# A conv-sequence block with two attentions: the order of the time-score products, and the shape of two band-score blocks

## The chip, the core and the metric

The kernel runs on one core of a Trainium2 chip. The metric is the device time of one execution in microseconds, the median of several runs. The core has a matrix engine (PE, with its weight loads shown as PEld), a vector engine (DVE), a scalar engine (ACT), GpSimd (POOL) and a queue that starts transfers (SP). PE works on 128x128 cells, and a product may use a part of them: a tile of rows*columns. "32*64" is a tile of 32 rows (the depth of the product) and 64 columns (the partitions of its output).

## The reference, cut to what matters

The input x has the shape (2, 256, 128, 128): batch, time, band, channel, in float32. Two attentions with 4 heads of depth 32 follow each other, the first over the 256 times with a causal mask, the second over the 128 bands with a mask that leaves |i - j| <= 16. A feed-forward block ends it.

```
xt = ln(x, ...).transpose(0, 2, 1, 3)
x = x + mha(xt, t_wi, ..., h=4, mask=causal(256)).transpose(0, 2, 1, 3)
xf = ln(x, ...)
x = x + mha(xf, f_wi, ..., h=4, mask=band(128, 16))
xn = ln(x, ...)
x = x + (gelu(xn @ w1.T + b1) @ w2.T + b2)

# inside mha
scores = einsum('...hqd,...hkd->...hqk', q, k) / sqrt(32) + mask
o = einsum('...hqk,...hkd->...hqd', softmax(scores), v)
```

## The kernel before, in words

The work is cut into groups of 512 rows, `NT = 4` blocks of 128. There are 128 groups of time attention (`OverTime`, two sequences of 256 times each), then 128 of band attention (`OverBands`, four sequences of 128 bands) and 128 of feed-forward, the last two in alternating runs of eight. `BoundedPath.run` (line 1058) is a hand-written software pipeline: one turn of its loop issues pieces of several groups, and every engine executes what it is given in this order (`InOrder` pins it).

A time step issues on PE: the scores (`time_scores`), the row sums and weighted values of an earlier group (`weigh`: `p,ones` and `p,v`), the output product of a still earlier one (`output`: `wn,oT`), the queries and keys (`xnT,wf`) and the values (`wf,xnT`) of a later one. A band step has the same parts with `pf` in place of `p`.

Scores are made transposed, keys on partitions and queries along the free dimension, one product per head and half block of 64 keys. The row group of PE is the head (its 32 rows), the column half is that of the output's partitions; so there are eight 32*64 tiles, and products on different tiles can run beside each other. `first_scores` (line 678) makes, for a new group, the scores of the first 128 keys of a sequence against all 256 queries from the key on: 256 queries for the first half of the keys, 192 for the second. `second_scores` (line 686) makes, for the group before it, the second 128 keys against the second 128 queries: 64 and 128 queries, with the halves exchanged, so that each tile gets 256 + 64 or 192 + 128 columns per head and sequence. `time_scores` (line 741) interleaves both by a written list of head, kind and sequence, with both halves of each entry one after the other; 32 products in all.

Each head's scores have a bank of their own in PSUM: `a0` to `a3` for the first scores, `b0` to `b3` for the second. In a step these banks come from other work. After the exchange at the end of the loop's body (lines 1164 to 1169), `b1` is the bank that held the weighted values `op` of the step before, which DVE reads last (`oT`), and `b2` is the one with the new values `vp`, which ACT copies to `v`. `rp`, the row sums, is written into `b0` after the scores, when ACT has read the second scores of head 0 from it. ACT takes the exponentials in the order: second scores of heads 0 and 3, first scores of head 1, second of 1 and 2, first of 2, and later first of 0 and 3.

`OverBands.scores` (line 764) goes over the four sequences `i` and two halves `e` of 64 keys, and over the heads innermost: 32 products of 64 keys by 80 queries (the half and the 16 bands beside it), each on a 32*64 tile. What lies outside of the band is masked after the exponential, or before it for one head.

PE takes each float32 product in two passes, so that every product leaves two loads and two matmuls in the profile, and the counts there are twice those of the code.

Of the kernel before, what the change touches and what calls it, by code (L numbers as in the profile page):

```python
# [19 lines left out]
P = 128  # L20
H = 4
D = 32
BAND = 16
EPS = 1e-5
NEG = -1e38
NT = 4
# [6 lines left out]
HALF = P // 2  # L33
# [613 lines left out]
def rows_of(h):  # L647
    return slice(h * D, (h + 1) * D)
# [9 lines left out]
class OverTime(Attention):  # L658
# [16 lines left out]
        self.p1 = path.work.tile([P, 2, H, 2, P], F32, name="p1", tag="h", bufs=2)  # L675
        self.s1 = {h: path.bank([P, 2, P], "sp", path.banks[f"b{h}"]) for h in range(H)}

    def first_scores(self, h, s):
        r, a = rows_of(h), 2 * s * P
        for e in range(0, P, HALF):  # L680
            self.path.tensor.matmul(
                self.s0[h][e : e + HALF, s, e:], self.kT[r, a + e : a + e + HALF], self.qT[r, a + e : a + 2 * P],
                start=True, stop=True,
            )

    def second_scores(self, h, s):
        r, a = rows_of(h), (2 * s + 1) * P
        for e in range(0, P, HALF):
            q = P - HALF - e
            self.path.tensor.matmul(  # L690
                self.s1[h][e : e + HALF, s, q:], self.kT[r, a + q : a + q + HALF], self.qT[r, a + q : a + P],
                start=True, stop=True,
            )

    def first_weights(self, heads):
        for h in heads:
# [41 lines left out]
        self.rp = rp.rearrange("p s n q -> p (s n q)")  # L738


def time_scores(old, new):


    if new is not None:
        new.first_tiles()
    if old is not None:
        old.second_tiles()
    for h, second, s in (
        (0, 1, 0), (1, 0, 0), (2, 0, 0), (3, 1, 0), (0, 1, 1), (3, 1, 1), (0, 0, 0), (3, 0, 0),
        (1, 0, 1), (2, 0, 1), (0, 0, 1), (3, 0, 1), (1, 1, 0), (2, 1, 0), (1, 1, 1), (2, 1, 1),  # L750
    ):
        if second and old is not None:
            old.second_scores(h, s)
        if not second and new is not None:
            new.first_scores(h, s)


class OverBands(Attention):
# [5 lines left out]
    def scores(self, heads):  # L764
        path = self.path
        self.sp = {h: path.bank([P, NT * P], "sp") for h in heads}
        for i in range(NT):
            for e in range(2):
                keys = slice(e * HALF, (e + 1) * HALF)
                a = i * P + e * (HALF - BAND)  # L770
                q = slice(a, a + HALF + BAND)
                for h in heads:
                    r = rows_of(h)
                    path.tensor.matmul(
                        self.sp[h][keys, q], self.kT[r, i * P + e * HALF : i * P + (e + 1) * HALF], self.qT[r, q],
                        start=True, stop=True,
                    )

    def first_function(self):
# [107 lines left out]
class BoundedPath:  # L887
# [170 lines left out]
    def run(self, x, out):  # L1058
# [21 lines left out]
        for n in range(-12, len(groups) + 2):  # L1080
# [10 lines left out]
            if old is not None or new is not None:  # L1091
                time_scores(old, new)
                b = self.banks
                Attention.place = dict(rp=b["b0"], op=b["b3"], yp=b["a1"], qp=b["a2"], kp=b["b1"], vp=b["b2"])
            else:
                Attention.place = {}
# [142 lines left out]
```

## Time and profile before

| | |
|---|---|
| median of 3 runs | 2707.29 us (2706.91 to 2709.16) |
| the profiled execution | 2709.79 us |
| its span, first to last instruction | 2708.0 us |
| time stage | up to about 980 us |
| band and feed-forward stage | from there to the end |
| `bank<-qT,kT`, all scores | 16384 matmul records, of them 8192 with 80 columns |
| mean of one record of 64, 80, 128, 192, 256 columns | 223, 244, 277, 331, 386 ns |

The page has the span, the busy time of each engine and its share, and the groups of instructions. "Busy" of PE counts the time in which at least one matmul is in flight, and a record runs from the start of a matmul to its end in the pipe; records of several tiles overlap. A timeline merges instructions that follow each other with the same operands: start, length, engine, line, operation, output and inputs, tile, shape, count, and in brackets the idle time before it and what ended it. Line 882 is the helper through which every pinned instruction goes, so groups are told apart by tile names.

### The profile page before, as it was taken

What the parts mean: (1) busy time and instruction counts of PE and PEld (TensorE: products, weight loads), DVE (VectorE), ACT (ScalarE), POOL (GpSimd) and SP (SyncE); (2) the same over time, 40 slices, a digit from 0 to 9 for tenths busy, and PEclk for the clock granted to TensorE, in tenths of its full rate; (3) what the DMA queues carried; (4) which work ended last, traced back from release to release, by engine and by line L of the source; (5) the groups of instructions that cost most, each with busy time, mean ns of one, the idle gap of its engine ahead of it and who ended that gap; (6) DMA issues with size and microseconds to landing.
All of it is one profiled execution on the core that took longest, in us unless ns stands there. A gap on an engine that the chain in (4) does not pass through costs nothing.

```text
span 2708.0 us, 156754 instructions
## 1 busy us (share of the span) xinstructions
PE 2670.3 (99%) x68662; PEld 1826.6 (67%) x68662; DVE 2176.8 (80%) x6708; ACT 1858.2 (69%) x3620; POOL 1952.8 (72%) x2297
## 2 busy tenths in 40 slices
PE   8999999999999999999999999999999999999998
PEld 5766666666766666666666666666666667666665
DVE  7888888888888898868779678687697796886974
ACT  6888888888888874755746647557456465575563
POOL 4888888888888887667657666676576666665762
PEclk9999999999999999999999999999999999999999
DMA  5555555555555535445454454454444444544533
GB/s 147 152 148 145 149 148 141 150 146 146 150 141 149 145 95 137 109 117 135 106 127 124 114 130 110 120 133 111 124 126 113 124 118 120 130 113 123 128 100 82
DMA packets 471513, 347.10 MB, mean 128 GB/s; under 512 B 43297, under 2 KB 405153, under 8 KB 470817
## 3 DMA queue, kind: packets, MB, share of 16 engines
q1 hardware_dynamic: 469568, 335.92, 48.2%
q8 instruction: 540, 8.85, 1.5%
q14 instruction: 157, 1.28, 0.2%
q10 hardware_dynamic: 1248, 1.05, 0.1%
HBM read 169.03 MB, written 167.77 MB: 124 GB/s over the span
## 4 chain that ended last, share of the span: by engine, by line
PE 81%; DVE 14%; DMA 2%; issue 1%; SPq 1%; ACT 0%; DVEq 0%; ACTq 0%
PE bank L882 81%; DVE xh L882 3%; DVE bank L882 3%; DVE z L882 2%; DVE stats L882 2%; DVE u L882 2%; DVE x L882 1%; DMA xnT<-turned 1%; DVE mv L882 1%; DMA turned<-z 1%; SPq L882 1%; DMA x<-in_x 0%; DVE oT L882 0%; DMA rows_sb<-in_rows 0%; ACT p L882 0%
## 5 line engine op out<-in xcount | busy, mean ns | idle before, releaser
L882 ACT ACTIVATE hT<-bank,b 128x512 f32<-128x512 f32 x512 | 347.0, 688 | 535.8 <-PE bank L882 517.7
L882 POOL TENSOR_SCALAR_AFFINE_SELECT pf<-pf 128x512 f32<-128x512 f32 x768 | 478.6, 637 | 248.1 <-ACT pf L882 221.7
L882 DVE TENSOR_SCALAR xh<-x,mv,rstd 128x160 f32<-128x160 f32 x1536 | 596.9, 431 | 14.3
L882 PEld LDWEIGHTS bank<-w2T_sb,hT 128*32 128x32 f32 x16384 | 459.7, 110 | 63.3 <-issue 39.7
L882 PE MATMUL bank<-xnT,wf 128*32 128x512 f32 x4096 | 489.1, 592 | 2.5 <-ACT p L882 2.5
L882 PE MATMUL bank<-w2T_sb,hT 128*32 128x128 f32 x16384 | 477.7, 273 | 1.1 <-issue 0.8
L882 PE MATMUL bank<-xnT,w1f 128*32 128x512 f32 x4096 | 474.8, 592 | 0.0
L882 DVE TENSOR_TENSOR res<-bank,res 128x512 f32<-128x512 f32 x256 | 175.9, 687 | 338.9 <-PE bank L882 337.7
L882 POOL TENSOR_SCALAR_AFFINE_SELECT p<-p 128x1024 f32<-128x1024 f32 (+2 forms) x384 | 364.8, 950 | 109.9 <-ACT p L882 101.4
L882 ACT ACTIVATE p<-bank 128x512 f32<-128x512 f32 (+1 forms) x1024 | 417.4, 499 | 21.7 <-PE bank L882 4.1
L882 PE MATMUL bank<-qT,kT 32*64 32x80 f32 (+4 forms) x16384 | 351.7, 274 | 3.7 <-DVE oT L882 2.4
L882 PEld LDWEIGHTS bank<-wf,xnT 128*32 128x32 f32 x8192 | 236.0, 110 | 153.9 <-issue 101.2
L882 PEld LDWEIGHTS bank<-qT,kT 32*64 32x64 f32 x16384 | 295.7, 130 | 58.9 <-ACT kT L882 48.0
L882 POOL TENSOR_TENSOR p<-p,p 128x512 f32<-128x512 f32 x256 | 324.1, 1287 | 10.7
L882 DVE BATCH_NORM_STATS2 stats<-x 128x6 f32<-128x128 f32 x1536 | 326.5, 275 | 0.6 <-DMA x<-in_x 0.6
L882 ACT ACTIVATE pf<-bank 128x512 f32<-128x512 f32 x512 | 267.0, 602 | 50.9 <-PE bank L882 48.9
L882 PEld LDWEIGHTS bank<-xnT,w1f 128*32 128x32 f32 x4096 | 156.4, 110 | 189.9 <-issue 160.3
L882 DVE STREAM_TRANSPOSE z<-xh 128x512 f32<-128x512 f32 x384 | 273.3, 712 | 13.5
L882 POOL TENSOR_SCALAR rstd<-mv 128x4 f32<-128x4 f32 x248 | 56.7, 229 | 311.7 <-DVE mv L882 310.3
L882 PE MATMUL bank<-wn,oT 128*32 128x128 f32 x8192 | 273.2, 273 | 0.0
L882 PE MATMUL bank<-wf,xnT 128*32 128x128 f32 x8192 | 273.0, 273 | 0.0
L882 POOL TENSOR_TENSOR rstd<-rstd,mhalf 128x4 f32<-128x4 f32 x248 | 257.0, 1036 | 20.7
(97 smaller groups left out, 3656.3 us busy)
## 6 DMA issues: line engine op xcount, KB each, us to landing
turned<-z SPq DMA_DIRECT2D x1536, 64.0 KB, 2.5
xnT<-turned SPq DMA_DIRECT2D x384, 256.0 KB, 3.2
x<-in_x SPq DMA_DIRECT2D x128, 256.0 KB, 4.4
x<-res SPq DMA_DIRECT2D x256, 128.0 KB, 2.4
x<-x SPq DMA_DIRECT2D x128, 256.0 KB, 4.3
out<-res SPq DMA_DIRECT2D x256, 128.0 KB, 2.5
w1T_sb<-in_w1T ACTq DMA_DIRECT2D x1, 256.0 KB, 6.6
w2T_sb<-in_w2T ACTq DMA_DIRECT2D x1, 256.0 KB, 8.0
```

Of the source, the lines that this page charges most:

```text
L882: return self.tc.keep_in_program_order(emit(*args, **kwargs))
```

## The change

Two things change. The time scores are issued one half at a time, by a list `TIME_ORDER` of 32 entries: the kind (`s` second, `f` first), the head, the sequence and the half. The products are the same as before, only their order differs: the two halves of a pair no longer stand side by side, and the kinds are mixed differently.

In the band scores, the first and last sequence keep their products of 64 keys by 80 queries. The second and third become one product per head of 128 keys by 128 queries each, over all 128 columns of PE (a 32*128 tile). So a group has 24 products in place of 32: 8, then 4 and 4 whole ones, then 8.

```diff
-    def first_scores(self, h, s):
+    def first_scores(self, h, s, e):
         r, a = rows_of(h), 2 * s * P
-        for e in range(0, P, HALF):
-            self.path.tensor.matmul(
-                self.s0[h][e : e + HALF, s, e:], self.kT[r, a + e : a + e + HALF], self.qT[r, a + e : a + 2 * P],
-                start=True, stop=True,
-            )
...
+        self.path.tensor.matmul(
+            self.s0[h][e : e + HALF, s, e:], self.kT[r, a + e : a + e + HALF], self.qT[r, a + e : a + 2 * P],
+            start=True, stop=True,
+        )
+
+    def second_scores(self, h, s, e):
+        r, a, q = rows_of(h), (2 * s + 1) * P, P - HALF - e
+        self.path.tensor.matmul(
+            self.s1[h][e : e + HALF, s, q:], self.kT[r, a + q : a + q + HALF], self.qT[r, a + q : a + P],
+            start=True, stop=True,
+        )
...
+TIME_ORDER = """
+    s010 s011 s310 s301 s300 f111 f110 s000 s001 f311 f211 f210 f300 f201 f101 f010
+    f011 f200 f100 f310 s311 s111 f000 s201 f001 s110 f301 s101 s211 s200 s100 s210
+""".split()
...
-    for h, second, s in (
-        (0, 1, 0), (1, 0, 0), (2, 0, 0), (3, 1, 0), (0, 1, 1), (3, 1, 1), (0, 0, 0), (3, 0, 0),
-        (1, 0, 1), (2, 0, 1), (0, 0, 1), (3, 0, 1), (1, 1, 0), (2, 1, 0), (1, 1, 1), (2, 1, 1),
-    ):
-        if second and old is not None:
-            old.second_scores(h, s)
-        if not second and new is not None:
-            new.first_scores(h, s)
+    for kind, h, s, e in TIME_ORDER:
+        if kind == "s" and old is not None:
+            old.second_scores(int(h), int(s), int(e) * HALF)
+        if kind == "f" and new is not None:
+            new.first_scores(int(h), int(s), int(e) * HALF)
...
-        for i in range(NT):
-            for e in range(2):
-                keys = slice(e * HALF, (e + 1) * HALF)
-                a = i * P + e * (HALF - BAND)
-                q = slice(a, a + HALF + BAND)
+        for i, part in ((0, HALF), (1, P), (2, P), (3, HALF)):
+            reach = 0 if part == P else BAND
+            for e in range(0, P, part):
+                a = i * P + (e - reach if e else 0)
+                q, keys = slice(a, a + part + reach), slice(i * P + e, i * P + e + part)
                 for h in heads:
                     r = rows_of(h)
                     path.tensor.matmul(
-                        self.sp[h][keys, q], self.kT[r, i * P + e * HALF : i * P + (e + 1) * HALF], self.qT[r, q],
-                        start=True, stop=True,
+                        self.sp[h][e : e + part, q], self.kT[r, keys], self.qT[r, q], start=True, stop=True
                     )
```

The other engines and the transfers get the same instructions in the same order as before.

More of the change, by code (lines that the diff above doesn't have):

```diff
@@ L676, in second_tiles @@
         self.s1 = {h: path.bank([P, 2, P], "sp", path.banks[f"b{h}"]) for h in range(H)}
-    def first_scores(self, h, s):
+    def first_scores(self, h, s, e):
         r, a = rows_of(h), 2 * s * P
-        for e in range(0, P, HALF):
-            self.path.tensor.matmul(
-                self.s0[h][e : e + HALF, s, e:], self.kT[r, a + e : a + e + HALF], self.qT[r, a + e : a + 2 * P],
-                start=True, stop=True,
-            )
[L686 to L691, printed above, removed]
-                start=True, stop=True,
-            )
+        self.path.tensor.matmul(
[8 more added lines that the diff above has]
+        )
     def first_weights(self, heads):
@@ L774, in scores @@
                     path.tensor.matmul(
-                        self.sp[h][keys, q], self.kT[r, i * P + e * HALF : i * P + (e + 1) * HALF], self.qT[r, q],
-                        start=True, stop=True,
+                        self.sp[h][e : e + part, q], self.kT[r, keys], self.qT[r, q], start=True, stop=True
                     )
```

## The prediction, made before the changed kernel ran

> **What bounds the kernel now.** I read the page first, then the timeline of TensorE (PE) in both stages, then the weight loads of one group of score products in slices, then ScalarE's timeline beside it.
>
> ```profile
> PE 2670.3 (99%) x68662; PEld 1826.6 (67%) x68662; DVE 2176.8 (80%) x6708; ACT 1858.2 (69%) x3620; POOL 1952.8 (72%) x2297
> ```
>
> PE has no idle time that counts; but a busy PE isn't a full one. The timeline of PE (start, length, tiles as rows*columns, records) shows what a step is made of:
>
> ```profile
> 501.87 1.90 PE L882 MATMUL bank<-xnT,wf 128*32 128x512 f32 x16
> 503.59 1.06 PE L882 MATMUL bank<-wf,xnT 128*32 128x128 f32 x32
> 504.57 1.66 PE L882 MATMUL bank<-qT,kT 32*64 32x64 f32 x64
> 506.16 1.07 PE L882 MATMUL bank<-p,ones 128*32 128x256 f32 x16
> ...
> 511.93 1.66 PE L882 MATMUL bank<-qT,kT 32*64 32x64 f32 x64
> ...
> 1214.61 1.06 PE L882 MATMUL bank<-qT,kT 32*64 32x80 f32 x64
> 1215.61 1.06 PE L882 MATMUL bank<-pf,ones 128*32 128x512 f32 x8
> ```
>
> A time step lasts 511.93 - 504.57 = 7.36 us, its scores 506.16 - 504.57 = 1.59 us (1.588 in the records, within 2 ns in nearly every step). A band group's scores take 1.00 us here; over all 128 groups of the trace 1.02 in the mean, 0.90 to 1.11 in most. Every product has two records (a load and a stream each): 32 products are 64 records. Sixteen records of 512 columns over four column tiles take 503.59 - 501.87 = 1.72 us, so a tile needs 0.43 us for 512 columns, 0.84 ns a column and record, 1.67 ns a column and product. On each of the eight 32*64 tiles the time scores stream 640 columns: 1.07 us. With 0.05 for the first load and 0.09 of emptying at the end, 1.21 would do; 0.38 us of each step is lost. The loads of the score products, sliced (busy time, count), show where:
>
> ```profile
> 504.77:504.87 0.10, 0.10 (x16) 1.00 0.75 164
> 504.87:504.97 0.10, 0.10 (x13) 1.00 0.88 184
> 504.97:505.07 0.10, 0.10 (x11) 1.00 0.74 164
> 505.07:505.17 0.10, 0.10 (x8) 1.00 1.05 256
> 505.17:505.27 0.10, 0.08 (x5) 1.00 0.74 185
> 505.27:505.37 0.10, 0.10 (x10) 1.00 0.98 225
> ```
>
> Loads thin out and stop before 505.26. Single records say why. Counted from the group's first load, the 18th, 19th and 20th products load at 0.356, 0.467, 0.687; the 1st, 2nd and 3rd end (with all ahead of them) at 0.326, 0.437, 0.656. A product enters 0.03 us after the one 17 places before it is retired in order. The third is a 256-column product, so all that follows waits for it while tiles stand empty. After that they enter 16.7 ns apart.
>
> **The Trainium skill.** "TensorE: Matmul & The Clock Gate", table at the top: the queue is 64 deep with partial reordering. It agrees: 64 records of load and stream are 16 products, one more is at the door. The same page, Part 3, has matmuls start in strict order; here they don't across tiles (the second stream of the 7th product starts at 0.149, that of the 3rd at 0.282). "TensorEngine Tiling (Array Packing)", Key Properties: "Changing tiling mode (not just tile) drains the TensorE". The trace agrees, also where only the column width changes. The last 128*128 stream, of 384 columns, starts at 27.674 and so ends at 27.994; the first load of 128*32 comes at 28.088, 0.094 later, where loads within one mode run ahead:
>
> ```profile
> 28.09 0.16 PEld L882 LDWEIGHTS bank<-xnT,wf 128*32 128x32 f32 x8 [0.55 <-issue]
> ```
>
> Its operand's fetch was issued at 22.31 (median landing 3.2 us later), so this isn't the wait. The step from values to scores costs 0.093 in the same way.
>
> **Time scores: gain.** The new list issues the same 32 products; nothing else moves, and the other engines keep their order. I replay both lists by rules taken from these records: eight tiles as queues, 1.67 ns a column, the second load hidden, entry at the 17th predecessor's retirement plus 0.03, 16.7 ns apart, a tile accepting one further product behind a started one. The old list comes out at 1.585 (trace 1.588). The new one gives 1.30 without waits. But bank b2 holds the previous values until ScalarE has copied them, as its timeline shows:
>
> ```profile
> 504.71 0.59 ACT L882 COPY v<-bank 128x512 f32<-128x512 f32 x1 [0.29 <-PE bank L882]
> 505.44 2.19 ACT L882 ACTIVATE p<-bank 128x256 f32<-128x256 f32 x6
> ```
>
> The copy ends 0.73 after the first load. `s201`, 24th of 32, is the first to write b2, and in an in-order entry the eight products behind it wait too. Entry at 0.80 gives 1.376, at 0.83 (when the old list's first b2 product loaded) 1.406. A semaphore update may add 0.026. I take 1.40: 1.588 - 1.40 = 0.19 us in each of 127 full steps, **-24 us** (19 to 27). A second floor lies close: the first `p,ones` product overwrites b0, which ScalarE reads until 505.83; PE's wait on it passed at 505.864 and the next load needs 0.075 more, 1.37 after the start. Does the gain survive in the step? The tile with the latest move is head 3's second scores (`s311` is 21st): in the replay they end at 0.83, with 0.16 of pipe behind, and ScalarE takes them at 1.15 today. All other exponentials come later still. The engines' load in this stage, from the view by windows (busy us of PE, PEld, DVE, ACT, POOL):
>
> ```profile
> 500.00:600.00 100.00, 99.98 (x2604) 69.30 (x2600) 84.92 (x269) 88.73 (x204) 89.63 (x83) 1.00 0.55 146
> 1300.00:1500.00 200.00, 197.95 (x5176) 134.47 (x5172) 160.90 (x480) 120.81 (x200) 132.54 (x184) 1.00 0.48 121
> ```
>
> POOL, the fullest, has 0.896 x 7.36 = 6.6 us of work for a step that becomes 7.17. The query and key copies wait for PE (0.17 us each in ScalarE's timeline), so they move with it. I charge nothing; if POOL's or ScalarE's chain did bind, it would eat part of the 0.19.
>
> **Band scores: loss.** Before: 32 products of 80 columns, four on each tile, 0.53 us of streaming; the replay gives 0.895, the shortest burst of the trace 0.896; the mean of 1.02 holds some more steps of 0.026, which I put to semaphore updates between late entries. After: 8 products of 80 columns on 32*64 tiles, then 8 of 128 columns on 32*128 tiles, then 8 on 32*64. A whole product occupies both column tiles of its row group, so a row group streams 133 + 213 + 213 + 133 = 693 ns rather than 533. The width changes twice inside the group. Each drain costs 0.09, then a load lies open: 64 columns take 0.053 (stream held back that long at each group's start), 128 columns 0.107 at the same rate. Sum: load 0.053, stream 0.133, stagger of eight tiles 0.047; drain 0.09, load 0.107, stream 0.427, stagger 0.02; drain 0.09, load 0.053, stream 0.133, stagger 0.047; last drain 0.09: 1.29; the replay says 1.30. What is saved is the entry stall, as only 24 products pass. 1.30 - 1.02 = 0.28 us in 128 groups, **+36 us** (30 to 44). PE is the bound here too (second line above, 197.95 of 200), so it counts in full; only of the 12.0 us that PE waits for DVE at 16 turns (view of waits) a little may cover it. The trace has no 32*128 tile. Its price is bound from below by the case without a drain (0.94 a group, a gain; next part), from above by two semaphore steps more (1.36, 44 us). I take the drain, because both the page and the one change of width alone in the trace have it.
>
> **Sum.** -24 + 36 = +12 us on a profiled execution of 2709.8 us (span 2708.0 and 1.8 around it), 2721.5. The median of the runs is 2.5 lower: 2719.
>
> **Rivals.**
> - *No drain between 32-row widths* (not slower). Then a whole product need only wait for its two tiles, loads stay hidden and the group takes 0.94 in the replay: 0.08 x 128 = -10, with -24 together -34: 2673. For it: the row split stays as it is, and no such change lies in the trace. Against it: the 0.094 above, where also the rows stayed. It decides once a change costs under about 0.06 with its open load. Chance 0.13.
> - *A cheaper change*: the streams wait for each other, but no emptying: 1.12, +13 - 24 = -11: 2696. Chance 0.08.
> - *The order gains little*: the b2 or b0 wait resolves later than I put it, or the rule of 17 is another one that the old list merely fits. Time scores then stay within 0.05 of 1.59: 0 to -6, 2707 + 36 - 3 = 2740. For it: the first b2 product is the 24th in the new list and was the 27th. Against: three entries agree with the rule to 1 ns. Chance 0.12.
>
> **How the numbers follow.** The forecast has 0.67; its own range is 2710 to 2732 (-27 + 30 to -19 + 44). 0.2% is 5.4 us, about what a measurement here can tell from no change. Slower by more: 0.62 of the forecast's 0.67 and the third rival, 0.74; faster: the first two, 0.21; within: 0.05. The range 2690 to 2742 leaves out the first rival and the far ends, under 2 in 10.
>
> **What would show it.** Timeline: from the first `qT,kT` to `p,ones` 1.40 in a time step, from `qT,kT` to `pf,ones` about 1.30 in a band group, split in three by gaps. A step of about 7.17 us. I'm wrong if whole products follow the half ones without a gap, or if the time scores stay at 1.59.

## The result, and the profile after

The median of 22 runs is 2711.32 us, against 2707.96 us for 22 runs of the kernel before. The ratio is 1.001, with a 95% interval of 1.0004 to 1.0017: slower by about 3 us. The forecast was 2719, slower by more than 0.2%; the sign holds, the size doesn't.

Two large effects stand behind this small number. The timeline of PE in the time stage of the changed kernel (start, length, tiles, records; what a piece of work takes is counted from its start to the start of the next one):

```profile
500.24 1.42 PE L881 MATMUL bank<-qT,kT 32*64 32x64 f32 x64
501.59 1.07 PE L881 MATMUL bank<-p,ones 128*32 128x256 f32 x16
...
507.35 1.42 PE L881 MATMUL bank<-qT,kT 32*64 32x64 f32 x64
```

The scores of a step take 1.35 us in place of 1.59, and a step 507.35 - 500.24 = 7.12 us (7.116 in the records) in place of 7.352. In the band stage the same view shows:

```profile
1206.45 1.37 PE L881 MATMUL bank<-qT,kT 32*64 32x80 f32 x48
1207.76 1.06 PE L881 MATMUL bank<-pf,ones 128*32 128x512 f32 x8
...
1213.09 1.38 PE L881 MATMUL bank<-qT,kT 32*64 32x80 f32 x48
```

A band group's scores take 1.305 us, to within 4 ns in most groups, where the mean was 1.018 before. The stages are separated by the first band scores. Before the change they come at

```profile
976.83 0.97 PE L882 MATMUL bank<-qT,kT 32*64 32x80 f32 x64
```

and after it at

```profile
952.73 1.38 PE L881 MATMUL bank<-qT,kT 32*64 32x80 f32 x48
```

So the time stage gave 24.1 us, and the rest of the span grew from 1731.1 to 1757.1, by 26.0. But 128 groups x 0.287 us are 36.7, and the score times summed over all groups of the two traces, with the few groups of the first run that wait in both, are 130.4 and 169.0, 38.7 apart. Of the missing 11 to 13 us, 11.1 are in the view of waits: what PE waited for, in total us, times, and the longest. Before:

```profile
PE bank L882 <- DVE u L882: 12.0, 16, 0.8
```

After:

```profile
PE bank L881 <- DVE u L881: 0.9, 4, 0.3
```

At each of the 16 turns from band groups to feed-forward groups PE had waited some 0.75 us for DVE, which makes `u`, a step of the division by the row sums. Nearly all of this wait is gone: 11.1 us of the longer scores lie where PE stood still before.

### The profile page after: what moved, and what is told of

Its sections match the earlier page's. It is cut to its first block, busy times and chain, and to the rows that moved or that the text cites. A ratio compares the mean times of both kernels' runs of the same rounds, so it can differ in the third digit from the quotient of the medians.

```text
span 2709.8 us, 152534 instructions
## 1 busy us (share of the span) xinstructions
PE 2682.0 (99%) x66614; PEld 1805.8 (67%) x66614; DVE 2195.4 (81%) x6708; ACT 1854.5 (68%) x3620; POOL 1952.3 (72%) x2297
## 4 chain that ended last, share of the span: by engine, by line
PE 87%; DVE 10%; DMA 1%; ACT 1%; issue 0%; POOL 0%; SPq 0%; DVEq 0%; ACTq 0%
PE bank L881 87%; DVE xh L881 2%; DVE bank L881 2%; DVE stats L881 1%; DVE u L881 1%; DVE z L881 1%; DVE x L881 1%; DVE oT L881 1%; DMA xnT<-turned 1%; DVE mv L881 0%; DMA x<-in_x 0%; ACT p L881 0%; DVE vy L881 0%; DMA rows_sb<-in_rows 0%; DVE res L881 0%
## 5 line engine op out<-in xcount | busy, mean ns | idle before, releaser
L881 ACT ACTIVATE p<-bank 128x512 f32<-128x512 f32 (+1 forms) x1024 | 430.7, 494 | 38.4 <-PE bank L881 27.2
L881 PE MATMUL bank<-qT,kT 32*64 32x80 f32 (+5 forms) x14336 | 363.5, 288 | 3.8 <-DVE oT L881 2.4
L881 PEld LDWEIGHTS bank<-qT,kT 32*64 32x64 f32 (+1 forms) x14336 | 288.8, 138 | 85.5 <-ACT kT L881 49.0
L881 PEld LDWEIGHTS bank<-xnT,w1f 128*32 128x32 f32 x4096 | 150.5, 110 | 193.9 <-issue 168.7
```

The lines of the kernel that those rows point to most:

```text
L881: return self.tc.keep_in_program_order(emit(*args, **kwargs))
```

## The experiments

The first four runs take the change apart and ask what the band products cost. The ten runs were measured in three sets (the first four, the next four, the last two), in which the kernel before took 2708.86, 2708.16 and 2708.19 us; differences between sets are uncertain by about 1 us more.

**The time order alone**: the band scores are those of before, `TIME_ORDER` stays. Against the changed kernel:

```diff
-        for i, part in ((0, HALF), (1, P), (2, P), (3, HALF)):
...
+        for i in range(NT):
+            for e in range(2):
+                keys = slice(e * HALF, (e + 1) * HALF)
...
```

> The new order of the time scores alone, the band scores as before. Theory A (the two parts act in their own stages, and the time order gains what the trace after shows, 0.236 us a step, less 5 us at the ends of the stage): -24, so 2684 (2680 to 2686); a time step of 7.12 us, and PE waits for DVE u again by about 12 us. Rival B (the time order gains little of its own, and the difference to the forecast lies in the bands alone): 2700 or more.

Measured: 2683.32 us, ratio 0.9907 (0.9891 to 0.9924). PE waits for DVE as before the change:

```profile
PE bank L882 <- DVE u L882: 12.7, 17, 0.8
```

In PE's timeline the wait stands in front of the row sums, here at the first turn:

```profile
1006.79 1.07 PE L882 MATMUL bank<-pf,ones 128*32 128x512 f32 x8 [0.78 <-DVE u L882]
```

The time order is worth 25.5 us by itself.

**The whole products alone**: the time scores of before. Against the kernel before:

```diff
-        for i in range(NT):
-            for e in range(2):
+        for i, part in ((0, HALF), (1, P), (2, P), (3, HALF)):
+            reach = 0 if part == P else BAND
+            for e in range(0, P, part):
...
```

> The whole products in the band scores alone, the time order as before. Theory A (DVE lags behind PE in each run of eight band groups, and the first 0.7 us by which PE's steps get longer in a run are free): a group's scores take 1.305 us, 0.287 more; 128 of them 36.7, less the 11 us by which PE's waits for DVE u shrink: +26, so 2734 (2732 to 2736), PE waits for DVE u under 2 us. Rival B (nothing covers it, the forecast's step): +36, 2744, with the wait for DVE u still 12 us.

Measured: 2736.38 us, ratio 1.01 (1.0083 to 1.0116), 27.5 us more than before; the scores of a group take 1.305 us again, and the wait is

```profile
PE bank L881 <- DVE u L881: 0.6, 3, 0.2
```

-25.5 and +27.5 leave +2.0, where both together measured +3.4; the parts act each in its stage and add up to within 2 us. Rival B, that nothing covers the bands' loss, is out.

**One change of width in a group**, against the changed kernel:

```diff
-        for i, part in ((0, HALF), (1, P), (2, P), (3, HALF)):
+        for i, part in ((0, HALF), (3, HALF), (1, P), (2, P)):
```

> The changed kernel with the band sequences in the order 0, 3, 1, 2: halves first, then the whole products, so the width changes once inside a group in place of twice. Theory A (each change of width costs an emptying of 0.09 us, an open load and a new stagger): a group's scores 1.305 - 0.19 = 1.11 us, 0.094 over before; 8 x 0.094 = 0.75 us a run, just what DVE's lag covers: the time of the time order alone, 2684, within 3. Rival B (the price lies in the streams of the whole products, not in the changes): 1.25 to 1.3 us, 2705 or more.

**No change of width in a group**:

```diff
-        for i, part in ((0, HALF), (1, P), (2, P), (3, HALF)):
+        for i, part in ((0, P), (1, P), (2, P), (3, P)):
```

> The changed kernel with all four band sequences as whole products: 16 products of 128 queries on 32*128 tiles, no change of width inside a group. Theory A (the price is the changes of width): load 0.107, four streams of 0.213, stagger 0.02, emptying 0.09: 1.07 to 1.09 us a group, 2682 (2679 to 2686). Rival B (whole products are dear in themselves, twice the columns of a half on each tile): over 1.3 us, slower than the changed kernel.

Measured: 2690.13 us (0.9932, 0.9915 to 0.9948) and 2690.70 us (0.9931, 0.9914 to 0.9947). The groups take 1.119 and 1.103 us; here is one of each in PE's timeline, first of the run with one change:

```profile
1209.01 1.19 PE L881 MATMUL bank<-qT,kT 32*64 32x80 f32 x48
1210.12 1.07 PE L881 MATMUL bank<-pf,ones 128*32 128x512 f32 x8
```

and of the run with none:

```profile
1205.07 1.17 PE L881 MATMUL bank<-qT,kT 32*128 32x128 f32 x32
1206.18 1.07 PE L881 MATMUL bank<-pf,ones 128*32 128x512 f32 x8
```

The price is that of the changes of width, not of the whole products: four whole products for each head, which put more columns on every tile than any other variant, take 0.2 us less than the mixture. But both runs are 7 us over the time order alone, where theory A had them even. Their groups are 0.10 and 0.085 us longer than before, 13 and 11 us in all, and the wait for DVE shrank by some 5 only. In the run with one change it is:

```profile
PE bank L881 <- DVE u L881: 6.9, 17, 0.6
```

So a longer group isn't covered wherever it stands in a run, and theory A, which put the two runs at 2684 and 2682, fell in this point. A new one, A': only the last groups before the turn count.

**Whole products in two groups of a run**, the first two or the last two. The place in the run is handed to the group, and decides the part of the middle sequences:

```diff
+        w = P if self.in_run in (0, 1) else HALF
-        for i, part in ((0, HALF), (1, P), (2, P), (3, HALF)):
+        for i, part in ((0, HALF), (1, w), (2, w), (3, HALF)):
```

(with `(6, 7)` in the other run).

> The changed kernel with whole products only in the first two band groups of each run of eight, halves in the other six. Two groups longer by 0.287 us in 16 runs: 9.2 us. Theory A (DVE's lag grows over the whole run, so any group covers): 2683 to 2685, PE's wait for DVE u falls from 12 to about 3 us. Theory A' (only the last groups of a run, whose chain through DVE ends at the turn, cover; the one-change run fits this, its wait fell by 5 us only): 2692 to 2693, the wait stays at 12.

> The same with whole products only in the last two band groups of each run. Theories A and A': 2683 to 2686, the wait for DVE u falls to 3 or 4 us. Rival B (no cover, the wait shrinks for another reason): 2692 to 2693.

Measured: 2694.11 us (0.9949, 0.9932 to 0.9965) with the first two, and 2683.37 us (0.9906, 0.9889 to 0.9922) with the last two. The time order alone has 2683.32 (its executions lie between 2682.15 and 2685.86, those of the last two between 2682.14 and 2686.64). The same products, as many and as long, cost 10.8 us at the start of a run and nothing that can be told from zero at its end. The waits, with the first two:

```profile
PE bank L882 <- DVE u L882: 12.8, 17, 0.8
```

and with the last two:

```profile
PE bank L882 <- DVE u L882: 4.3, 17, 0.4
```

**Is it DVE's work that PE waits for?** DVE's clamp and mask of the fourth head is cut to 32 of 128 queries, and the other 96 stay unmasked, with halves and with whole products (the time order is the new one in both):

```diff
-                sp, sp, LIMIT, path.band.unsqueeze(1).to_broadcast([P, NT, P]), ALU.min, ALU.add
+                sp[:, :, 0:D], sp[:, :, 0:D], LIMIT, path.band[:, 0:D].unsqueeze(1).to_broadcast([P, NT, D]),
+                ALU.min, ALU.add
```

> New time order, band scores in halves, and DVE clamps and masks the fourth head over 32 of each 128 queries only (the other 96 are left unmasked), which takes some 0.45 us from DVE in each band group. If DVE's chain at the turn is what PE waits for there, the wait for DVE u goes from 12 us to under 3 and the time from 2683 to 2671 to 2675. If that wait follows something else and DVE only comes last: 2683.

> The changed kernel with the same shorter clamp and mask (96 of 128 queries of the fourth head are left unmasked). With no wait for DVE left to cover anything, the band change should cost its full 36 us against the halves with the short mask (2708 to 2711), where it costs 27 to 28 with DVE's full work. If the cover is not DVE: again 27 to 28 more.

Measured: 2666.21 us (0.9843, 0.9826 to 0.9859) and 2705.23 us (0.9987, 0.998 to 0.9995). In both, one wait of 0.3 us for DVE `u` is left, and none at a turn. With halves:

```profile
PE bank L883 <- DVE u L883: 0.3, 1, 0.3
```

and with whole products:

```profile
PE bank L882 <- DVE u L882: 0.3, 1, 0.3
```

The band change then costs 39.0 us, no less than the 36.7 to 38.7 by which its groups are longer, where it cost 28.0 (2711.32 - 2683.32) beside DVE's full work. The cover was DVE's chain. Both runs came out below their expected ranges, by 5 and 3 us. The gain with halves is 17.1 us, and the wait that went is 12.4 of them. Some 3 more are in the score groups, which from the fifth group on sum to 122.2 us rather than 125.3. More than half of these lie in the last group of a run, and are again a wait for DVE: in 14 of the 16 runs of the time order alone the load of its third product comes 0.06 to 0.23 us late, behind DVE's `x<-bank,x`, and with the short mask in none. The view of PE's waits can't show this, as the first two products are still in flight. The last 1.6 us stay open.

**A version from this**: the time order, halves, and in the last two groups of a run POOL masks the fourth head too, as it does the other three, so that DVE's 0.69 us fall away there. In a second run the same in every other group.

```diff
+                    group.by_vector = 0 if j in (6, 7) else 1
```

> New time order, band scores in halves, and in the last two groups of each run of eight POOL masks all four heads, so that DVE's clamp and mask of the fourth head (0.69 us) falls away there and POOL gets two selects more (1.28 us). Theory A' (DVE's chain in the last groups sets the wait at the turn): the wait for DVE u falls from 12 us to under 4, the time from 2683 to 2672 to 2677. Rival: POOL, with some 1.2 us free in a band step, falls behind at the turn and PE waits for it instead: 2683 or more.

> The same for every other group of a run (2nd, 4th, 6th, 8th). Theory A': about as the last two, 2670 to 2677, as one of the last two and one before are relieved, and DVE has 1.4 us less in four steps. Rival: POOL falls behind: 2683 or more.

Measured: 2671.08 us (0.986, 0.9844 to 0.9876) and 2679.63 us (0.9894, 0.9878 to 0.9911). The first is 37 us under the kernel before, the fastest of all complete ones here. In both, 0.3 us of the wait for DVE `u` are left. The second missed its range of 2670 to 2677: PE's timeline at the first turn has a new wait, in front of the fourth head's row sums:

```profile
1011.01 0.62 PE L882 MATMUL bank<-pf,ones 128*32 128x512 f32 x1 [0.25 <-POOL pf L882]
```

and the third step of a run takes 6.88 us in place of 6.29 in the mean of the 16 runs (time order alone), which is 9.4 us in all. There too, in the records of two of these steps, the load for the fourth head's row sums stands 0.46 us behind POOL's `pf`. POOL doesn't keep up everywhere it was given the work.

## Why the prediction was wrong, step by step

**The entry rule of the time scores: borne out; the gain of a step too small, the total by luck.** The replay gave 1.376 for an entry of `s201` at 0.80. In the records of the changed kernel `s201` loads at 0.776 and the group takes 1.352; my replay gives the same with 0.776 put in, but this is after the fact, and no run tests the rule of 17 apart from the order. The third rival, scores within 0.05 of 1.59, is out. I had moved the number up to 1.40 with a later entry and a semaphore update that didn't come; that the steps of 0.026 in the trace are semaphore updates no run here shows. So the gain is 0.236 in a steady step, which would be 30.0 in 127, not 24. That the traces give 24 all the same is luck: some 6 us are lost, most of them near the ends of the stage, which I hadn't counted. The first steps are not bound by PE: ScalarE is behind there, and PE's wait before the third `xnT,wf` grew from 1.40 us before to 1.89:

```profile
40.03 3.41 PE L881 MATMUL bank<-xnT,wf 128*32 128x512 f32 x16 [1.89 <-ACT p L881]
```

(The 3.41 where other profiles have 1.92 goes with a granted clock of 0.55 from 40 to 43 us in this one execution; its 1.5 us, and 0.9 us by which the first scores begin later here, are of the 6.) At the end, the last step, with second scores alone, begins 6.18 rather than 4.87 us after the one before it.

**The second floor, `b0`: there, lower than I put it, and not decisive.** I had it at 1.37. PE's wait for ScalarE's reading of `b0` passed at 1.235 after the group's first load, the next load could follow 0.075 later at 1.31, and the emptying ended at 1.352.

**The price of a changed width: right, in its size too.** 1.30 was worked out, 1.305 measured. In a group's records the last stream of the halves ends at 0.235 and the first whole load is at 0.324, 0.089 later; the whole products' last stream ends 0.092 before the next half load. The load lies open for 0.107 as taken. What the Trainium skill says in "TensorEngine Tiling (Array Packing)", Key Properties, that a change of tiling mode drains TensorE, is borne out for a change between 32*64 and 32*128, which no trace had shown; the rivals without a drain (0.94) or without emptying (1.12) are out.

**"PE is the bound here too (second line above, 197.95 of 200), so it counts in full; only of the 12.0 us that PE waits for DVE at 16 turns (view of waits) a little may cover it": wrong.** This is the step that failed. Nearly all of the wait covered it, 11 of 12 us. The view had shown the sum and the number of these waits; what I hadn't asked is how much later they would end if PE's groups before them became longer. A mean of PE's busy time over the stage says nothing of that, and neither does DVE's, which was 160.90 of 200 us in the same line. Within a run of band groups DVE's timeline before the change shows what the mean hides, by its mask of the fourth head:

```profile
1215.89 0.70 DVE L882 SCALAR_TENSOR_TENSOR bank<-bank,band 128x512 f32<-128x512 f32 x1 [0.74 <-PE bank L882]
...
1222.44 0.69 DVE L882 SCALAR_TENSOR_TENSOR bank<-bank,band 128x512 f32<-128x512 f32 x1
...
1228.97 0.69 DVE L882 SCALAR_TENSOR_TENSOR bank<-bank,band 128x512 f32<-128x512 f32 x1
```

In the fourth group DVE waits for PE, and in 14 of the 16 runs this is its last idle time of over 0.1 us before the turn. From there on it needs 6.53 us a group, where PE takes about 6.33, and falls behind by some 0.2 us in each: from a group's first score to its mask it is 1.28 us in the fourth group and 2.11 in the eighth (medians of the 16 runs). This lag is what PE waits out at the turn. In the changed kernel PE's own step is 6.64 us, DVE keeps up, and the mask comes at 1.66 in every group from the second on.

So only the groups after DVE's last wait for PE can be longer for nothing, and only up to its lag. The experiments fit: the last two groups, longer by 0.57 us a run, cost nothing; in the first two, where DVE still waits for PE and moves with it, the same cost 10.8 us. In the run with one change the wait fell by 0.36 us a turn, about the 0.40 of four groups. Four groups of 0.287 us are 1.15 us, more than the 0.75 of a wait, so the wait is used up. With 36 - 11 the sum would have been -24 + 25 = +1, and the measured +3 is within a few microseconds of it.

**Other engines: nearly right.** ScalarE did get a new wait in each step, which I had excluded. Its six exponentials ran in one piece (x6) before, and now break after the first:

```profile
501.05 0.38 ACT L881 ACTIVATE p<-bank 128x256 f32<-128x256 f32 x1
501.61 1.92 ACT L881 ACTIVATE p<-bank 128x256 f32<-128x256 f32 x5 [0.18 <-PE bank L881]
```

It begins head 3's second scores 501.61 - 500.24 = 1.37 us after the first load, where I had them ready at 0.99. In the steady steps the wait is hidden: they got shorter by as much as the scores.

## What to carry to other kernels

Before charging a longer piece of work in full to a saturated engine, look at the places where this engine waits for another one, and at how that other one fares in the pieces ahead: those in which it works without a pause can become longer for nothing, up to the wait; those in which it still waits for the saturated engine can't. A mean over a stage hides both. Where many small products share the array, count from the records how many may enter behind a long one, and replay the order; rules taken from one trace foretold 1.376 us for a quite different order that took 1.352. Before mixing tile widths inside a burst of short products, price the changes: taking one of two out of a group here saved 0.19 us of 1.305.

## What the hardware showed beyond that

The records fit a rule that a finished product is made known in program order. In those of the changed kernel the last product of head 3's second scores, 21st of 32, ends at 0.99 us after the group's first load, but a first-score product one place ahead of it ends at 1.32 only. The semaphore that tells of the former is updated at 1.35, and ScalarE starts at 1.37. (Ends of products are modelled in the profile; the update and ScalarE's start are not.) An early place on a tile was no use to the reader of the result here, with a long product ahead of it in the list.
